# A message-passing graph layer: node features in three DMAs a chunk, loaded three chunks ahead of the stores of h, and the first edge scalars behind the last store

## The chip, the cores and the metric

The kernel runs on one core of one Trainium2 chip. The metric is device time in microseconds (us), from the first to the last instruction with the launch's own share around it; the median of three runs is given with the lowest and the highest. The engines are named as in the profile: PE multiplies matrices, DVE and ACT do elementwise work, POOL here issues gathers, and SP only issues DMAs. SP, ACT and POOL each have a queue of DMAs, and these run on 16 DMA engines.

## The reference

One equivariant graph layer with 12500 nodes and 400000 edges, a residual, and a layer norm over each node's 160 features:

```python
s = node_features[:, :64]; v = node_features[:, 64:].reshape(n, 32, 3); a = node_attr
sc_s = s @ sc_ws * a * _inv(64)
sc_v = jnp.einsum('nci,cd->ndi', v, sc_wv) * a[:, :, None] * _inv(32)
h_s = s @ lin1_ws * a * _inv(64)
h_v = jnp.einsum('nci,cd->ndi', v, lin1_wv) * a[:, :, None] * _inv(32)
hid = jax.nn.silu(edge_scalars @ fc_w1 * _inv(64))
w = hid @ fc_w2 * _inv(64)
w1, w2, w3, w4, w5 = jnp.split(w, [64, 128, 160, 192], axis=-1)
es, ev = h_s[edge_src], h_v[edge_src]            # gathers by edge
e0, e1 = edge_attr[:, :1], edge_attr[:, 1:4]
mid_s = [w1 * es * e0,  w4 * (ev . e1) * _inv(3)]
mid_v = [(w2 * es) e1,  w3 ev e0,  w5 cross(ev, e1) * _inv(2)]
agg = segment_sum(mid, edge_dst) / sqrt(16)
o = agg through lin2_ws, lin2_wv, times a
scalars, gates = silu(pre_s[:, :64]), sigmoid(pre_s[:, 64:96])    # pre = sc + o
x = _layernorm(x + concat([scalars, gates * pre_v]))
```

The edges come sorted by destination. All arithmetic is in float32.

## The kernel before, in words

Constants, then a **node stage**, then an **edge stage** of 782 steps of four tiles (a tile is 128 edges), with the finishing of nodes threaded into it.

The node stage (L252 to L342) computes h, 160 values for each node, and stores it to the table `h_tab` in device memory, from which the edge stage gathers. It goes in chunks of 2048 nodes (`CH`): six whole ones and one of 212. The features come transposed: `xs_t` has 64 rows of scalars, `xv_t` 96 rows of vector components. The tile `xa` holds 64 rows of scalars and the first 64 of the vectors (128 partitions by 2048 nodes); `xz` holds the last 32 rows, with the chunk's four quarters one under another (128 partitions by 512). A chunk loads in eight DMAs on SP's queue: `xa` in two halves of the nodes, each as 64 partitions from `xs_t` (L268) and 64 from `xv_t` (L269), 256 KB each, and `xz` in four of 32 partitions, 64 KB each (L273). All chunks have tiles of their own, so no load waits for a tile. PE multiplies by `l1` and `l1z` (L310, L325), DVE multiplies the products by the nodes' attribute into `ht` (L313, L328; three buffers), and ACT's queue stores `ht` to `h_tab` (L339, and L342 for the last 84 nodes). Ahead of chunk 3, `bases` (L286) turns the first destination of each block of three tiles (`rows`, L247, two DMAs at the front of SP's queue) into window starts `lo`.

The written order on SP is: `rows`; all loads of all chunks; the first source indices and edge attributes (L183, L184); the first chunk of edge scalars `es` (L222, two DMAs of 384 KB); the maps `w1` (L280) and `w2` in five pieces, both twice (L283); then `scs`, `scv` and 19 pieces of `l2` (L351, L118, L372). On ACT: the attribute `at`, `l1`, `l1z` and their scaling (L98 to L125), the stores of h, then all destinations `dt` (L345, 1.6 MB). On DVE, behind the node stage: the scaling of `w2` (L348), `rel` from `dt` and `lo` (L379, L384), and the scalings of `l2`, `scv` and `scs` (L110). In the built program the DMAs of SP and ACT share eight semaphores in turn, so each waits for the landing of the one eight places before it in the scheduled order of both queues.

The edge stage: a step gathers h for four tiles on POOL (L419, an indirect DMA for each tile, into one of four buffers `hg`), makes weights on PE from the edge scalars (L410, L412, L431), multiplies weights and gathered rows on DVE into `pr` (L441, L449), builds the selection from `rel` (L487, L490) and sums by destination on PE (L497). Products of a step need its gather, `hid` and, in DVE's order, `rel` before them.

`manual_schedule` keeps the written order on an engine; DMAs and DVE's scalings of the constants can still be placed among the edge stage's first steps.

Of the kernel before, what the change touches and what calls it, by code (L numbers as in the profile page):

```python
# [10 lines left out]
F32 = mybir.dt.float32  # L11
# [9 lines left out]
P = 128  # L21
S = 64
V = 32
# [5 lines left out]
BT = 3  # L29
# [10 lines left out]
NWT = 224  # L40
# [12 lines left out]
def gnn_kernel(  # L53
# [21 lines left out]
    nc = tc.nc  # L75
    N = x.shape[0]
    NT = attr.shape[1]
# [4 lines left out]
    NB = -(-TT // BT)  # L82
# [11 lines left out]
    in_order = ctx.enter_context(ExitStack())  # L94
    in_order.enter_context(tc.manual_schedule(
        engines={ENG.PE, ENG.DVE, ENG.Activation, ENG.Pool, ENG.SP}))
    at = consts.tile([P, NT], F32, name="at")
    nc.scalar.dma_start(at, attr)  # L98

    l1 = consts.tile([P, P], F32, name="l1")  # L100
    nc.vector.memset(l1, 0.0)
    nc.scalar.dma_start(l1[:S, :S], lin1_ws)
    for i in range(2):
        r = slice(S + i * V, S + (i + 1) * V)
        nc.scalar.dma_start(l1[r, r], lin1_wv)
    scales = [(l1[:S], 1.0 / math.sqrt(S)), (l1[S:], 1.0 / math.sqrt(V))]

    def scale():
        for m, by in scales:
            nc.vector.tensor_scalar_mul(m, m, by)  # L110
        scales.clear()

    def block_diagonal(name, w, n, scale, queue=nc.scalar):
        k = w.shape[0]
        m = consts.tile([n * k, n * k], F32, name=name)
        nc.vector.memset(m, 0.0)
        for i in range(n):
            queue.dma_start(m[i * k:(i + 1) * k, i * k:(i + 1) * k], w)  # L118
        if scale != 1.0:
            scales.append((m, scale))  # L120
        return m

    l1z = block_diagonal("l1z", lin1_wv, 4, 1.0 / math.sqrt(V))
    for m, by in scales:
        nc.scalar.mul(m, m, by)  # L125
    scales.clear()


    rel = consts.tile([P, TT], I16, name="rel")
    rows = consts.tile([1, NB], I32, name="rows")  # L130
    early = consts.tile([1, 1], F32, name="early")
# [58 lines left out]
    def index(t):  # L190
        a0, idx, _ = ahead(t)
        return idx[:, t - a0:t - a0 + 1]
# [13 lines left out]

    ess = {}

    def load_chunk(c):
        if c in ess:  # L210
            return
        t0, halves = chunks[c]
        es = ess[c] = loads.tile([2 * S, SIDE * P], F32, name="es")
        for half, n in enumerate(halves):
            to = es[half * S:(half + 1) * S]
            e0 = (t0 + half * BT) * P
            if n < BT:
                nc.sync.dma_start(to[:, :n * P], es_t[:, e0:e0 + n * P])
                continue
            k = n // BT  # L220
            full = es_t[:, e0:e0 + EB]
            nc.sync.dma_start(  # L222
                to[:, :n * P].rearrange("c (q e) -> c q e", e=EB),
                bass.AP(tensor=full.tensor, offset=full.offset,
                        ap=[full.ap[0], [2 * EB, k], [1, EB]]))
# [16 lines left out]
    nc.gpsimd.iota(share, pattern=[[RATE, NB]], base=0, channel_multiplier=0)  # L242

    even = NB // 16 * 16
    with nc.allow_non_contiguous_dma(reason="the first destination of each block"):
        for b0, b1, outer in ((0, even, 16), (even, NB, 1)):
            nc.sync.dma_start(  # L247
                rows[:, b0:b1].rearrange("o (a b) -> o a b", a=outer),
                dst[0:1, b0 * BT:(b1 - 1) * BT + 1:BT].rearrange("o (a b) -> o a b", a=outer))


    U = 4  # L252
# [2 lines left out]
    CH = 4 * U * P  # L255
    starts = list(range(0, N, CH))
    with tc.tile_pool(name="nodes", bufs=len(starts)) as nodes, tc.tile_pool(
        name="nodes_ps", bufs=6, space=PSUM
    ) as nps, tc.tile_pool(name="z_ps", bufs=2, space=PSUM) as zps:
        loaded = []  # L260
        for c0 in starts:
            cn = min(CH, N - c0)
            quarters = 4 if cn == CH else 1
            assert quarters == 4 or cn <= U * P
            xa = nodes.tile([P, CH], F32, name="xa")
            for b0 in range(0, cn, CH // 2):
                b1 = min(b0 + CH // 2, cn)
                nc.sync.dma_start(xa[:S, b0:b1], xs_t[:, c0 + b0:c0 + b1])  # L268
                nc.sync.dma_start(xa[S:, b0:b1], xv_t[:2 * V, c0 + b0:c0 + b1])  # L269
            xz = nodes.tile([P, U * P], F32, name="xz")  # L270
            cq = cn // quarters
            for q in range(quarters):
                nc.sync.dma_start(xz[q * V:(q + 1) * V, :cq],  # L273
                                  xv_t[2 * V:, c0 + q * cq:c0 + (q + 1) * cq])
            loaded.append((c0, cn, quarters, cq, xa, xz))
        index(0)
        load_chunk(0)
        for half in range(2):
            r = slice(half * S, (half + 1) * S)
            nc.sync.dma_start(w1[r, r], fc_w1)  # L280
            at_c = 0
            for a, b in ((64, 128), (0, 64), (192, 224), (160, 192), (128, 160)):
                nc.sync.dma_start(w2[r, at_c:at_c + b - a], fc_w2[:, a:b])  # L283
                at_c += b - a

        def bases():  # L286

            base_f = ends_pool.tile([1, NB], F32, name="base_f")
            nc.vector.tensor_copy(base_f, rows)
            for b0 in range(0, NB, U * P):  # L290
                b1 = min(NB, b0 + U * P)
                ps = nps.tile([P, U, P], F32, name="hp").rearrange("p u c -> p (u c)")
                nc.tensor.matmul(ps[:, :b1 - b0], ones, base_f[:, b0:b1], start=True, stop=True)
                nc.scalar.copy(lo[:, b0:b1], ps[:, :b1 - b0])
            nc.vector.tensor_sub(share, rows, share)
            nc.vector.tensor_reduce(early, share, AX.X, OP.min)
            nc.vector.tensor_scalar(early, early, -float(MARGIN), None, op0=OP.is_lt)

        for c0, cn, quarters, cq, xa, xz in loaded:
            if c0 == 3 * CH:  # L300
                bases()
            ht = nodes.tile([P, 4 * U, D], F32, name="ht", bufs=3)
            nt = -(-cn // P)
            first = c0 // P
            full = cn // P
            for t0 in range(0, nt, U):
                ps = nps.tile([P, U, P], F32, name="hp")
                for t in range(t0, min(t0 + U, nt)):
                    n = min(P, cn - t * P)
                    nc.tensor.matmul(ps[:n, t - t0], xa[:, t * P:t * P + n], l1,  # L310
                                     start=True, stop=True)
                k = min(U, full - t0)
                nc.vector.tensor_mul(  # L313
                    ht[:, t0:t0 + k, :P], ps[:, :k],
                    at[:, first + t0:first + t0 + k, None].to_broadcast([P, k, P]))
                if t0 + k < nt <= t0 + U:
                    n = cn - full * P
                    nc.vector.tensor_scalar(ht[:n, full, :P], ps[:n, full - t0],
                                            at[:n, first + full:first + full + 1], None, op0=OP.mult)

            pz = zps.tile([P, U, 4, V], F32, name="pz")
            k = quarters * V
            for u in range(-(-cq // P)):
                n = min(P, cq - u * P)
                nc.tensor.matmul(pz[:n, u, :quarters].rearrange("p q c -> p (q c)"),  # L325
                                 xz[:k, u * P:u * P + n], l1z[:k, :k], start=True, stop=True)
            if quarters == 4:
                nc.vector.tensor_mul(  # L328
                    ht[:, :, P:].rearrange("p (q u) c -> p u q c", q=4), pz,
                    at[:, first:first + 4 * U].rearrange("p (q u) -> p u q", q=4)[:, :, :, None]  # L330
                    .to_broadcast([P, U, 4, V]))
            else:
                nc.vector.tensor_mul(ht[:, :full, P:], pz[:, :full, 0],
                                     at[:, first:first + full, None].to_broadcast([P, full, V]))
            if cn > full * P:
                n = cn - full * P
                nc.vector.tensor_scalar(ht[:n, full, P:], pz[:n, full, 0],
                                        at[:n, first + full:first + full + 1], None, op0=OP.mult)
            nc.scalar.dma_start(  # L339
                h_tab[c0:c0 + full * P, :].rearrange("(q p) d -> p q d", p=P), ht[:, :full])  # L340
            if cn > full * P:
                nc.scalar.dma_start(h_tab[c0 + full * P:c0 + cn, :], ht[:n, full])  # L342


    nc.scalar.dma_start(dt, dst)  # L345
    iota = consts.tile([P, W], F32, name="iota")
    nc.vector.tensor_copy(iota, iota_i)
    nc.vector.tensor_scalar_mul(w2, w2, 1.0 / math.sqrt(64))  # L348

    scs = consts.tile([S, V3], F32, name="scs")  # L350
    nc.sync.dma_start(scs, sc_ws)  # L351
# [593 lines left out]
```

## Time and profile before

| | us |
|---|---|
| median of 3 runs | 4070.39 |
| lowest, highest | 4069.28, 4070.66 |
| the profiled execution | 4073.52 |
| its span, first to last instruction | 4071.7 |
| PE busy | 3355.0 (82%) |
| POOL busy | 3011.1 (74%), 3125 gathers in it |
| DVE busy | 2431.4 (60%) |
| ACT busy | 957.8 (24%) |
| DVE's last product of the node stage ends | 71.3 |
| first gather begins | 79.10 |
| first product of the edge stage (L441) begins | 93.93 |

The page gives the busy time of each engine, and for each group of instructions what its engine's idle time before it waited for. A timeline's line is: start, duration, engine, line, operation, tiles, count, and in brackets the idle time before it and what ended that. "SPq" and "ACTq" are the issuing of DMAs on these queues. A DMA's bytes move later than its issue.

### The profile page before, as it was taken

The page shows a single profiled execution, that of the slowest core. Times are in us where ns is not written, and L with a number is a line of the kernel's source. Part 1 is how long each engine was busy: PE and PEld are TensorE (multiplying, and loading weights), DVE is VectorE, ACT ScalarE, POOL GpSimd, SP SyncE. Part 2 cuts the span into 40 slices and gives each one's busy share as a digit, 9 for nine tenths or more (in the row PEclk, how much of TensorE's full clock was granted, in tenths as well). Part 3 has the DMA queues.
Part 4 walks back from the last instruction along what each step waited for, and adds up shares of the span by engine and source line. Part 5 has one row for each costly group of instructions (what it writes and reads, how often), then busy time and mean ns, then how long its engine had stood idle before and what let it go on. Part 6 is the DMA issues. An engine that isn't in the chain of part 4 may idle for free. (4 is left out here: it accounts for less than half of the span.)

```text
span 4071.7 us, 54463 instructions
## 1 busy us (share of the span) xinstructions
PE 3355.0 (82%) x17415; PEld 1636.2 (40%) x17415; DVE 2431.4 (60%) x6367; ACT 957.8 (24%) x3033; POOL 3011.1 (74%) x3133
## 2 busy tenths in 40 slices
PE   5888888887888888888888888888888888888887
PEld 4343443443443433434344343344343343444443
DVE  4655665665655656656656566566565665655655
ACT  0312222221222222222222122122222221221222
POOL 1777777777777777777777777777777777777775
PEclk7989889999998998998999899999899998998988
DMA  8434444444434434434444344344444444444442
GB/s 206 113 90 101 101 97 98 105 93 101 106 91 109 100 91 109 100 90 109 96 94 109 93 100 107 93 101 102 96 101 97 100 101 99 100 100 100 98 97 58
DMA packets 293165, 412.20 MB, mean 101 GB/s; under 512 B 75694, under 2 KB 240442, under 8 KB 292746
## 3 DMA queue, kind: packets, MB, share of 16 engines
q0 software_dynamic: 150000, 256.20, 26.2%
q1 hardware_dynamic: 129592, 142.75, 15.9%
q10 hardware_dynamic: 13282, 9.69, 0.8%
q8 instruction: 143, 2.34, 0.2%
q14 instruction: 148, 1.21, 0.1%
HBM read 392.40 MB, written 16.00 MB: 100 GB/s over the span
## 5 line engine op out<-in xcount | busy, mean ns | idle before, releaser
L419 POOL DMA_INDIRECT hg<-h_tab,idx x3125 | 3009.4, 963 | 1028.5 <-issue 852.5
L441 DVE TENSOR_TENSOR pr<-pw,hg 128x512 f32<-128x512 f32 x782 | 539.3, 690 | 1497.5 <-DMA hg<-h_tab,idx 1191.6
L497 PE MATMUL pa<-pr,sel 128*64 128x416 f32 x6250 | 1407.0, 575 | 2.3 <-DVE sel L490 2.3
L431 PE MATMUL pw<-w,hid 64*128 64x224 f32 x6250 | 873.9, 395 | 481.9 <-DVE oh L487 449.3
L449 DVE TENSOR_TENSOR pr<-pw,hg 128x384 f32<-128x384 f32 x2346 | 1152.7, 546 | 0.1
L431 PEld LDWEIGHTS pw<-w,hid 64*128 64x128 f32 x6250 | 583.3, 197 | 789.5 <-issue 657.9
L497 PEld LDWEIGHTS pa<-pr,sel 128*64 128x64 f32 x6250 | 408.5, 146 | 599.5 <-issue 551.1
L690 ACT COPY sa<-pa 128x416 f32<-128x416 f32 x521 | 263.2, 505 | 1320.9 <-PE pa L497 1315.8
L410 PE MATMUL ph<-es,w 128*128 128x512 f32 (+1 forms) x784 | 466.4, 678 | 28.5 <-DMA w<-in_fc_w_dram 12.9
L412 ACT ACTIVATE hid<-ph 128x512 f32<-128x512 f32 x392 | 233.6, 596 | 765.6 <-PE ph L410 765.0
L490 DVE TENSOR_TENSOR sel<-oh,eas 128x256 f32<-128x256 f32 x782 | 337.9, 432 | 38.1 <-DVE oh L487 0.9
L506 PEld LDWEIGHTS pt<-ident,sa 128*128 128x128 f32 (+1 forms) x2084 | 222.2, 133 | 341.6 <-issue 255.2
L506 PE MATMUL pt<-ident,sa 128*128 128x128 f32 (+1 forms) x2084 | 336.1, 285 | 9.2 <-DVE acc L671 7.0
L522 PE MATMUL po<-tt,l 128*96 128x256 f32 (+3 forms) x1360 | 312.4, 377 | 12.8 <-DVE z L557 11.4
L510 ACT COPY tt<-pt 128x192 f32<-128x192 f32 x521 | 164.6, 316 | 525.3 <-PE pt L506 524.4
L522 PEld LDWEIGHTS po<-tt,l 128*96 128x96 f32 x1360 | 212.1, 164 | 129.5 <-issue 47.7
L410 PEld LDWEIGHTS ph<-es,w 128*128 128x128 f32 x784 | 126.2, 203 | 326.5 <-issue 249.1
L530 DVE TENSOR_TENSOR acc<-acc,os 96x32 f32 x1042 | 193.1, 185 | 24.7 <-ACT os L525 5.4
L487 DVE TENSOR_TENSOR oh<-rel,iota 128x64 f32<-128x64 int16 x782 | 168.7, 216 | 0.0
L556 PE MATMUL pp<-ident,acc 96*128 96x96 f32 x196 | 40.3, 294 | 127.7 <-DVE acc L530 127.0
L525 ACT COPY os<-po 96x512 f32<-96x512 f32 (+2 forms) x68 | 38.3, 564 | 311.9 <-PE po L522 298.7
L512 ACT COPY tt<-pt 128x32 f32<-128x32 f32 x521 | 102.5, 197 | 0.0
(78 smaller groups left out, 781.3 us busy)
## 6 DMA issues: line engine op xcount, KB each, us to landing
es<-in_es_t_dram SPq DMA_DIRECT2D x260, 384.0 KB
hg<-h_tab,idx POOLq DMA_INDIRECT x3125
h_tab<-ht ACTq DMA_DIRECT2D x6, 1280.0 KB
xt<-in_x_dram SPq DMA_DIRECT2D x23, 320.0 KB
out_dram<-y SPq DMA_DIRECT2D x23, 320.0 KB
xv<-in_xv_t_dram SPq DMA_DIRECT2D x25, 187.5 KB
eat<-in_ea_dram SPq DMA_DIRECT2D x30, 120.0 KB
xs<-in_xs_t_dram SPq DMA_DIRECT2D x25, 125.0 KB
```

The lines of the kernel that those rows point to most:

```text
L410: nc.tensor.matmul(ph[:k, c], w1[:k, :k], es[:k, t0 * P + c0 * P:t0 * P + c1 * P], start=True, stop=True)
L412: nc.scalar.activation(hid[:k, c], ph[:k, c], AF.Silu, scale=1.0 / math.sqrt(64))
L419: nc.gpsimd.indirect_dma_start(out=hg[:, t, :], out_offset=None, in_=h_tab, in_offset=bass.IndirectOffsetOnAxis(ap=i, axis=0))
L431: nc.tensor.matmul(pw[:, t, :NWT], hid[r, c * P:(c + 1) * P], w2[r], start=True, stop=True)
L441: nc.vector.tensor_mul(two, pw[:, :n, :2 * S].rearrange("p t (k c) -> p t k c", k=2), hg[:, :n, None, :S].to_broadcast([P, n, 2, S]))
L449: nc.vector.tensor_mul(pr[:, :n, first:first + V3].rearrange("p t (i c) -> p t i c", i=3), pw[:, :n, None, 2 * S + k * V:2 * S + (k + 1) * ...
L490: nc.vector.tensor_mul(sel[:, :n], oh[:, :, None, :].to_broadcast([P, n, 4, W]), by_slot(tiles[0][0])[:, u:u + n, :, None].to_broadcast([P ...
L497: nc.tensor.matmul(pa[half * ROWS:(half + 1) * ROWS, :NPR], sel[:, t].rearrange("p k w -> p (k w)"), pr, start=start, stop=stop)
L506: nc.tensor.transpose(pt[:c, four * P:four * P + k], sa[:k, four * P:four * P + c], ident[:k, :k])
L522: nc.tensor.matmul(po[:, k, :nb], l2[:b, terms[to, part, four]], a[:, :nb], start=(n == 0), stop=(n == len(of) - 1))
L530: nc.vector.tensor_add(window, window, os[:, :, b])
L690: nc.scalar.copy(sa, pas.pop(j)[:, :NPR])
```

## The change

The node stage's loads become a function, `load(c0)`, with three DMAs for each chunk: 64 partitions by 2048 from `xs_t`, 64 by 2048 from `xv_t` (512 KB each), and one of 128 partitions by 512 for `xz` (256 KB), whose side in device memory is an access pattern of 4 quarters by 32 rows by 512 values. Chunk 0 is loaded first of all, ahead of `at`, `l1` and `l1z`; then chunks 1 and 2, then `rows`; in the loop, chunk k + 3 is loaded ahead of the work and the store of chunk k. The first indices and attributes follow the last chunk's loads. `load_maps` loads `fc_w2` whole and twice into a tile `raw`, and DVE scales its five pieces into `w2`. The maps are loaded behind the node stage in the written order, and the first edge scalars go on ACT's queue, behind the last store of h and ahead of `dt`.

```diff
-    at = consts.tile([P, NT], F32, name="at")
-    nc.scalar.dma_start(at, attr)
...
-    l1z = block_diagonal("l1z", lin1_wv, 4, 1.0 / math.sqrt(V))
...
-    def load_chunk(c):
+    def load_chunk(c, queue=nc.sync):
...
-            nc.sync.dma_start(
+            queue.dma_start(
                 to[:, :n * P].rearrange("c (q e) -> c q e", e=EB),
...
-        for c0 in starts:
+
+        def load(c0):
+
             cn = min(CH, N - c0)
             quarters = 4 if cn == CH else 1
             assert quarters == 4 or cn <= U * P
             xa = nodes.tile([P, CH], F32, name="xa")
-            for b0 in range(0, cn, CH // 2):
-                b1 = min(b0 + CH // 2, cn)
-                nc.sync.dma_start(xa[:S, b0:b1], xs_t[:, c0 + b0:c0 + b1])
-                nc.sync.dma_start(xa[S:, b0:b1], xv_t[:2 * V, c0 + b0:c0 + b1])
+            nc.sync.dma_start(xa[:S, :cn], xs_t[:, c0:c0 + cn])
+            nc.sync.dma_start(xa[S:, :cn], xv_t[:2 * V, c0:c0 + cn])
             xz = nodes.tile([P, U * P], F32, name="xz")
             cq = cn // quarters
-            for q in range(quarters):
-                nc.sync.dma_start(xz[q * V:(q + 1) * V, :cq],
-                                  xv_t[2 * V:, c0 + q * cq:c0 + (q + 1) * cq])
+            z = xv_t[2 * V:, c0:c0 + cq]
+            nc.sync.dma_start(xz[:quarters * V, :cq],
+                              bass.AP(tensor=z.tensor, offset=z.offset,
+                                      ap=[[cq, quarters], [z.ap[0][0], V], [1, cq]]))
             loaded.append((c0, cn, quarters, cq, xa, xz))
-        index(0)
-        load_chunk(0)
-        for half in range(2):
-            r = slice(half * S, (half + 1) * S)
-            nc.sync.dma_start(w1[r, r], fc_w1)
-            at_c = 0
-            for a, b in ((64, 128), (0, 64), (192, 224), (160, 192), (128, 160)):
-                nc.sync.dma_start(w2[r, at_c:at_c + b - a], fc_w2[:, a:b])
-                at_c += b - a
+
+        def load_maps():
+
+            raw = ends_pool.tile([2 * S, NWT], F32, name="raw")
+            for half in range(2):
+                r = slice(half * S, (half + 1) * S)
+                nc.sync.dma_start(w1[r, r], fc_w1)
+                nc.sync.dma_start(raw[r], fc_w2)
+            return raw
...
-        for c0, cn, quarters, cq, xa, xz in loaded:
+        load(starts[0])
+        at = consts.tile([P, NT], F32, name="at")
+        nc.scalar.dma_start(at, attr)
...
+        for c0 in starts[1:3]:
+            load(c0)
+        load_bases()
+        for k, c0 in enumerate(starts):
+            if k + 3 < len(starts):
+                load(starts[k + 3])
+            elif k + 3 == len(starts):
+                index(0)
+            _, cn, quarters, cq, xa, xz = loaded[k]
             if c0 == 3 * CH:
                 bases()
...
+    raw = load_maps()
+    load_chunk(0, nc.scalar)
     nc.scalar.dma_start(dt, dst)
     iota = consts.tile([P, W], F32, name="iota")
     nc.vector.tensor_copy(iota, iota_i)
-    nc.vector.tensor_scalar_mul(w2, w2, 1.0 / math.sqrt(64))
+    at_c = 0
+    for a, b in ((64, 128), (0, 64), (192, 224), (160, 192), (128, 160)):
+        nc.vector.tensor_scalar_mul(w2[:, at_c:at_c + b - a], raw[:, a:b], 1.0 / math.sqrt(64))
+        at_c += b - a
```

In the built program of the changed kernel, SP's order behind the last chunk's loads is: indices, attributes, `w1` and `raw` twice, `scs`, the second indices and attributes, the first self-connection loads (`xs2`, `xv2`), `scv`, `l2`, the second chunk of edge scalars. On DVE all scalings of `scv`, `l2` and `scs` stand between `rel` and the first product, where before they were mixed into the products of the first steps. PE's and POOL's orders are unchanged.

More of the change, by code (lines that the diff above doesn't have):

```diff
@@ L96, in gnn_kernel @@
         engines={ENG.PE, ENG.DVE, ENG.Activation, ENG.Pool, ENG.SP}))
-    at = consts.tile([P, NT], F32, name="at")
-    nc.scalar.dma_start(at, attr)
[L100 to L121, printed above, removed]
-    l1z = block_diagonal("l1z", lin1_wv, 4, 1.0 / math.sqrt(V))
-    for m, by in scales:
-        nc.scalar.mul(m, m, by)
-    scales.clear()
     rel = consts.tile([P, TT], I16, name="rel")
@@ L217, in load_chunk @@
             if n < BT:
-                nc.sync.dma_start(to[:, :n * P], es_t[:, e0:e0 + n * P])
+                queue.dma_start(to[:, :n * P], es_t[:, e0:e0 + n * P])
                 continue
@@ L244, in gnn_kernel, with load_bases @@
     even = NB // 16 * 16
[L245 to L249, printed above, removed]
+    def load_bases():
+        with nc.allow_non_contiguous_dma(reason="the first destination of each block"):
+            for b0, b1, outer in ((0, even, 16), (even, NB, 1)):
+                nc.sync.dma_start(
+                    rows[:, b0:b1].rearrange("o (a b) -> o a b", a=outer),
+                    dst[0:1, b0 * BT:(b1 - 1) * BT + 1:BT].rearrange("o (a b) -> o a b", a=outer))
     U = 4
@@ L297, in bases, with scale, block_diagonal @@
             nc.vector.tensor_scalar(early, early, -float(MARGIN), None, op0=OP.is_lt)
-        for c0, cn, quarters, cq, xa, xz in loaded:
+        load(starts[0])
+        at = consts.tile([P, NT], F32, name="at")
+        nc.scalar.dma_start(at, attr)
+        l1 = consts.tile([P, P], F32, name="l1")
+        nc.vector.memset(l1, 0.0)
+        nc.scalar.dma_start(l1[:S, :S], lin1_ws)
+        for i in range(2):
+            r = slice(S + i * V, S + (i + 1) * V)
+            nc.scalar.dma_start(l1[r, r], lin1_wv)
+        scales = [(l1[:S], 1.0 / math.sqrt(S)), (l1[S:], 1.0 / math.sqrt(V))]
+        def scale():
+            for m, by in scales:
+                nc.vector.tensor_scalar_mul(m, m, by)
+            scales.clear()
+        def block_diagonal(name, w, n, scale, queue=nc.scalar):
+            k = w.shape[0]
+            m = consts.tile([n * k, n * k], F32, name=name)
+            nc.vector.memset(m, 0.0)
+            for i in range(n):
+                queue.dma_start(m[i * k:(i + 1) * k, i * k:(i + 1) * k], w)
+            if scale != 1.0:
+                scales.append((m, scale))
+            return m
+        l1z = block_diagonal("l1z", lin1_wv, 4, 1.0 / math.sqrt(V))
+        for m, by in scales:
+            nc.scalar.mul(m, m, by)
+        scales.clear()
+        for c0 in starts[1:3]:
[7 more added lines that the diff above has]
+            _, cn, quarters, cq, xa, xz = loaded[k]
             if c0 == 3 * CH:
```

## The prediction

> **What bounds the kernel now.** I read the page's groups first, then the waits of POOL over the whole span, then its timeline at both ends.
>
> ```profile
> L419 POOL DMA_INDIRECT hg<-h_tab,idx x3125 | 3009.4, 963 | 1028.5 <-issue 852.5
> ...
> POOL hg L419 <- issue: 852.5, 2798, 0.3
> POOL hg L419 <- DMA h_tab<-ht: 76.8, 1, 76.8
> POOL hg L419 <- DMA hg<-h_tab,idx: 34.4, 113, 0.3
> ...
> 79.10 1.10 POOL L419 DMA_INDIRECT hg<-h_tab,idx  x1 [76.75 <-DMA h_tab<-ht]
> 80.50 0.95 POOL L419 DMA_INDIRECT hg<-h_tab,idx  x1 [0.30 <-issue]
> ...
> 4039.35 0.94 POOL L419 DMA_INDIRECT hg<-h_tab,idx  x1 [0.30 <-DVE pr L449]
> ```
>
> PE is the busiest engine by share (82%), yet POOL sets the end: 3125 gathers follow each other with 0.3 us between them, and the longest wait of any kind behind the first is those 0.3 us. The one long wait is the first, 76.8 us for the stores of h. From the first gather (79.10) to the end of the last (4040.3) nothing holds POOL, and 31.4 us of tail follow. So whatever moves the first gather moves the end by as much, and nothing else in the first 80 us counts, unless it later makes POOL wait.
>
> What sets 79.10 is the DMA traffic of the node stage, which I read by windows (time, then engines' busy time, granted clock, DMA share, GB/s) and in the waits of SP's queue up to 110 us.
>
> ```profile
> 2.50:7.00 4.50, 0.00 (x0) 0.00 (x0) 0.04 (x1) 0.00 (x0) 0.00 (x0) 1.00 0.92 37
> 12.00:20.00 8.00, 7.54 (x45) 7.57 (x46) 3.11 (x5) 0.00 (x0) 0.00 (x0) 1.00 1.05 234
> 46.00:49.00 3.00, 3.00 (x19) 3.00 (x18) 1.25 (x2) 0.00 (x0) 0.00 (x0) 0.61 0.12 22
> 53.00:62.00 9.00, 5.26 (x36) 4.80 (x34) 3.46 (x5) 0.00 (x0) 0.00 (x0) 0.81 1.11 334
> 65.00:71.00 6.00, 5.51 (x32) 5.27 (x32) 2.45 (x6) 0.00 (x0) 0.00 (x0) 0.68 0.73 168
> ...
> SPq L268 <- DMA h_tab<-ht: 23.9, 3, 8.9
> SPq L283 <- DMA h_tab<-ht: 8.2, 1, 8.2
> SPq L269 <- DMA l<-in_lin_wv_dram: 5.8, 1, 5.8
> ```
>
> Loads run at 234 GB/s, a stretch of mostly stores at 334. The features are 12500 x 160 x 4 bytes = 8.0 MB in and h is 8.0 MB out: 34.2 + 24.0 us. The first edge scalars (2 x 0.39 MB, L222) take 3.4 us, indices and attributes (0.15 MB) 0.6. That is 62.2 us of full work. The other 16.9 us before the first gather are idle DMA: 8.3 in the first 10 us (0.40 MB moved, worth 1.7 us), 2.8 in 46 to 49 (3 us at 22 GB/s in place of 334), 1.7 in 65 to 71 (6 us at 168 in place of 234), some 2 from the last byte to the gather, 2.1 scattered. SP causes the holes: a load waits for the DMA eight places before it in the built order, and with eight loads a chunk that place is often a store.
>
> **The change, part by part, on the first gather's start.**
>
> *First edge scalars behind the last store.* They leave the path: -3.4 us. They now compete with the first gathers, which move 82 KB each 1.25 us (66 GB/s). Below it is asked whether they are late.
>
> *Destinations of blocks, and the start.* The two DMAs of L247 (1.41 us of SP) no longer stand ahead of the first features, and SP no longer waits 5.8 us at L269: the first chunk's two halves need no earlier DMA in the new order. The first row to bound it is 8.3 us lost; I take -4.5, ends 0 and -6.4 (2.21 to 8.58, from the first load's issue to the second's). Against it, L101's clearing of l1 stands behind the 0.94 us of L240, so PE's first product, at 12.46 waiting for xa, could then wait for l1: the 0 end holds that. Destinations are wanted at 39.41 (L289), 20 us behind their new place.
>
> *Three loads a chunk, three chunks ahead.* Eight DMAs in flight now span two chunks with their stores, and chunk 4 is the first load that must await a store (chunk 1's). The holes at 46 and 65 should close: -4.5, ends 0 and -6.6 (with the scattered 2.1). Joining halves (256 KB to 512 KB) changes no bytes: nothing, hidden in the queue.
>
> *Pulled ahead.* In the built order the second indices and attributes and the first self-connection loads (0.46 MB) now stand ahead of the last two stores, and chunk 6's stores wait for them by semaphore: 0.46 MB at 234 GB/s, +2.0; ends 0 and +4 (a further landing, 2 us).
>
> *The joined z load.* Four loads of 32 partitions become one, whose chip side counts 128 rows and whose memory side counts 4 quarters x 32 rows. On how many engines does it run? The page's row of ACT's queue (packets, MB, share) bears on it, and the DMA view of 40 to 50 us, in quarters of a us:
>
> ```profile
> q10 hardware_dynamic: 13282, 9.69, 0.8%
> ...
> GB/s 229 230 197 246 226 171 191 279 343 353 335 333 333 330 338 340 380 307 312 310 320 251 92 26 23 20 20 18 0 0 0 0 0 0 0 180 164 164 410 295
> ```
>
> ACT's 17 DMAs have 13012 pieces (at 128, l1 and l1z 256, stores 12288 + 128 + 84, destinations 128). 270 remain, which is 16 x 16 + 14 if each engine used posts one more: the 84-row store ran on 14 engines, the largest divisor of its rows up to 16. So row counts decide, and this load has two: by 128 it uses 16 engines, by 4 it uses 4. With four, these engines carry 64 KB of z a chunk in place of 16. In 45.75 to 47 a trickle of some 20 GB/s, a sixteenth of 334, is one straggling engine by itself: 48 KB more is 2.4 us a chunk, 14.4 for six. Against it, the four then lag, and their part of xa (64 KB at 234/16 = 14.6 GB/s, 4.4 us) runs beside idle neighbours at up to 20 GB/s, 3.2 us: -7.2. Net +7; ends 0 (16 engines) and +19.7 (48 KB at 14.6, no relief).
>
> The Trainium skill speaks against the change here: "DMA: Bandwidth & Descriptors", in the section on why a DMA increments its semaphore by 16, says that the number of engines is the largest up to 16 that divides the slowest dimension of both sides. The 14 above agrees, though there both sides had 84 rows. By that rule this load gets 4 engines and the sum is the forecast's; by the row alone 16 is as good a reading, and the sum is the first rival's.
>
> *Maps.* Ten loads of w2 become two of raw, and one product (L348, 0.28 us) five of at most that: DVE +1.1, while it waits for the destinations anyway. Without that cover, 1.1 at the first product.
>
> *What comes late behind the stores.* ACT now issues two edge-scalar loads and then dt, and by its semaphore dt also waits for one of the l2 loads that waits for the last full store: some 2.4 us (two issues, one landing) behind the last store, where before it was issued at 75.61, before the landing. Behind it stand all of DVE's work: rel, then all 20 scalings, now ahead of the first product where before they were mixed into it.
>
> ```profile
> 75.61 0.36 ACTq L345 DMA_DIRECT2D dt<-in_dst_dram  x1
> 86.40 0.28 DVE L348 TENSOR_SCALAR w<-w 128x224 f32<-128x224 f32 x1 [14.99 <-DMA w<-in_fc_w_dram]
> 86.70 7.05 DVE L379 TENSOR_TENSOR rel<-dt,lo 128x520 int16<-128x520 int32 x6
> 93.93 0.67 DVE L441 TENSOR_TENSOR pr<-pw,hg 128x512 f32<-128x512 f32 x1
> 102.29 0.94 POOL L419 DMA_INDIRECT hg<-h_tab,idx  x1 [0.31 <-DVE l L110]
> ```
>
> POOL has four gather buffers: the 17th gather needs the first product done. It is due 23.2 us behind the first gather (102.29 - 79.10), three gathers slowed beside rel included. The new chain, from the landing (1.4 us before the first gather, by POOL's first semaphore event at 77.7): 2.4, then 7 (1.6 MB at the 313 GB/s of 77 to 82, plus 2 for start and landing) to 11.1 (75.61 to 86.70), rel 7.5, scalings 4.6, product 2.4: 22.5 to 26.6 behind the first gather. A wait of 0 to 3.4 us, once. I take 0, as dt's bytes decide and L348 held rel before.
>
> **Sum.** 79.1 - 3.4 - 4.5 - 4.5 + 2.0 + 7.0 = 75.7: the first gather 3.4 us earlier. The profiled execution took 4073.5 (span 4071.7) and would take 4070.1; the median of the runs is 3.1 below it, so 4070.4 - 3.4 = 4067.0 us.
>
> **Rivals.** *The z load spreads over 16 engines.* First gather at 68.7 (the sum without the 7.0), 4060.0 us; with the far ends of start and holes and none of the 2.0 pulled ahead, 62.7 and 4054. For it: the 128 rows it writes, and that 270 shows a count of rows, not which side's. Against it: the 4.
>
> *The four z engines become the stage's bound.* Every chunk waits for the slowest engine, so the holes stay: 79.1 - 3.4 - 4.5 + 2.0 + 19.7 = 92.9, 4084.2 us, slower. It decides from the point where the four engines cost over 5.9 us while the holes stay (1.0 a chunk), or 10.4 where they close (1.7 a chunk); at 20 GB/s without relief they cost 2.4 a chunk. For it: loads at 14.6 GB/s an engine when all run. Against it: that rate belongs to 16 engines writing 64 partitions, not to four.
>
> *Late destinations give the gain back.* POOL waits 3.4 us before its 17th gather: 4070.4, no change. It decides where the first product ends over 23.2 us behind the first gather.
>
> **How the numbers follow.** Forecast 0.40, 16 engines 0.36, four engines as the bound 0.18, late destinations 0.06. What a measurement of this kernel tells from no change is about 0.2%, 8.1 us. Faster by more: 0.29 of the 16-engine case, and 0.13 of the forecast's, where the relief or the closed holes bring more: 0.42. Slower by more: 0.13 of the bound, 0.02 of the forecast's, 0.01 of late destinations: 0.16. The rest is 0.42. Range 4055 to 4078: the bottom is nearly the 16-engine case's best, the top holds half of the way into the four-engine bound. The forecast's own range is 4058 to 4074.
>
> **What would show it.** The first gather's start is the measure: 76 forecast, 63 to 69 with 16 engines, over 79 with the bound. The waits of SP for h_tab should shrink from 32 us, the window 2.5 to 7 fill up, and 46 to 49 hold no hole. Four engines show as a DMA rate near 80 GB/s (4 x 20) in stretches of the loads with the share far under 1. POOL should have no second wait over 0.3 us; one near the 17th gather is the destinations. It would all be wrong if POOL's step of 1.25 us changed.

## The result, and the profile after

The changed kernel takes 4083.88 us (median of 7 runs, 4081.34 to 4086.76) beside 4070.39 (4068.63 to 4075.97) for the kernel before in the same session: ratio 1.0033, 95% interval 1.0023 to 1.0043. It is slower by 13.5 us; 4067.0 was forecast, with 4078 as the top of the range. The profiled execution took 4083.88, its span is 4082.0 (before: 4071.7).

First the waits of POOL over the whole span: engine, tile, line, what it waited for, total us, times, longest.

```profile
POOL hg L434 <- issue: 857.8, 2816, 0.3
POOL hg L434 <- DMA h_tab<-ht: 86.0, 1, 86.0
POOL hg L434 <- DMA hg<-h_tab,idx: 33.2, 109, 0.3
POOL hg L434 <- DVE oh L502: 20.6, 53, 4.8
```

The first wait grew from 76.8 to 86.0 us, and there is a second one that is not 0.3 but 4.8. POOL's timeline places both:

```profile
88.38 1.10 POOL L434 DMA_INDIRECT hg<-h_tab,idx  x1 [86.03 <-DMA h_tab<-ht]
...
114.89 0.94 POOL L434 DMA_INDIRECT hg<-h_tab,idx  x1 [4.76 <-DVE oh L502]
...
4048.97 1.04 POOL L434 DMA_INDIRECT hg<-h_tab,idx  x1 [0.30 <-DVE oh L502]
```

The first gather starts at 88.38 in place of 79.10 (+9.3), and the 17th waits 4.76 us for the first products (the name in the bracket is the last of DVE's instructions by then). The last gather starts 9.6 us later than before. 13.7 us were lost and 4.1 came back on the way, mostly as shorter gathers: the busy time of the group L434 is 3005.6 us, that of L419 before was 3009.4. The step of 1.25 us is the same.

The windows of the node stage (time, busy time of PE, its weight loads, DVE, ACT and POOL, clock, DMA share, GB/s) show where the 9.3 us lie:

```profile
2.50:7.00 4.50, 0.00 (x0) 0.00 (x0) 0.06 (x1) 0.00 (x0) 0.00 (x0) 1.00 0.89 207
25.50:28.00 2.50, 2.50 (x25) 2.50 (x24) 1.53 (x3) 0.00 (x0) 0.00 (x0) 0.99 0.48 80
31.00:34.00 3.00, 1.15 (x5) 1.18 (x6) 0.00 (x0) 0.00 (x0) 0.00 (x0) 0.73 0.25 80
```

The start did fill: 207 GB/s from 2.5 to 7 us, where there were 37. But at 31 to 34 the DMA engines are busy a quarter of the time and move 80 GB/s: four of sixteen, 20 GB/s each, the sign that the forecast named. (25.5 to 28 is on the way there.) The waits of SP's queue up to 110 us, and ACT's queue:

```profile
SPq L238 <- DMA h_tab<-ht: 14.5, 1, 14.5
SPq L243 <- DMA h_tab<-ht: 13.5, 1, 13.5
SPq L243 <- DMA l<-in_lin_ws_dram: 6.5, 1, 6.5
```

```profile
19.64 24.60 ACTq L349 DMA_DIRECT2D h_tab<-ht  x3
44.29 1.15 ACT L265 COPY lo<-hp 128x512 f32<-128x512 f32 x3 [34.35 <-DMA h_tab<-ht]
```

Store 0 is issued at 19.64, and store 2 waits for its landing: the group of three stores ends at 44.2. A store of 1.3 MB thus needed some 24 us. The reading, which e1, e3 and e4 test: a quarter of its data goes through the four engines that also carry z, and it lands when those are done. The semaphore events of the trace, sixteen for each store, agree. Twelve of store 0's come at 27.2 to 28.7 us, the last four at 42.3 to 43.3, and store 2 is issued at 43.39. Store 1's come at 42.8 to 44.5 and 48.1 to 49.3, and chunk 4's loads, which waited 14.5 us for it, go at 49.34; store 3's come at 65.1 to 66.4 and 71.6 to 72.6, and chunk 6's z load, after 13.5 us, goes at 72.58.

The length of these waits is not the four engines' alone. In e1 below, with z on 16 engines, all sixteen events of store 0 come at 34.3 to 36.5, the last 19.8 us behind its issue, and SP's two long waits are 14.7 and 11.1 us; in the kernel before, store 0 landed 6.6 us behind its issue. So the stores are slower in the new order too, where more loads are queued ahead of them; no run parts this from the row load that now stands beside store 0.

The end of the stage, from the timelines of ACT and DVE (two views):

```profile
85.69 0.60 ACTq L352 DMA_DIRECT2D h_tab<-ht  x1
86.33 1.80 ACTq L190 DMA_DIRECT2D es<-in_es_t_dram  x2
93.20 0.36 ACTq L357 DMA_DIRECT2D dt<-in_dst_dram  x1
```

```profile
77.89 0.24 DVE L347 TENSOR_SCALAR ht<-pz,at 84x32 f32<-84x32 f32 x1
...
101.00 7.14 DVE L394 TENSOR_TENSOR rel<-dt,lo 128x520 int16<-128x520 int32 x6 [17.45 <-DMA dt<-in_dst_dram]
...
108.44 3.97 DVE L284 TENSOR_SCALAR l<-l 32x96 f32<-32x96 f32 x20
112.43 0.20 DVE L284 TENSOR_SCALAR scs<-scs 64x96 f32<-64x96 f32 x1
112.55 0.68 DVE L456 TENSOR_TENSOR pr<-pw,hg 128x512 f32<-128x512 f32 x1
```

DVE finishes h at 78.1, the last store is issued at 85.7, dt at 93.2 (75.61 before). rel starts at 101.0, the scalings follow, and the first products end at 114.6, 26.2 us behind the first gather, where the prediction allowed 23.2.

### The profile page after: what moved, and what is told of

Read it like the earlier page. It is cut to its first block, busy times and chain, and to the rows that moved or that the text cites. A ratio compares the mean times of both kernels' runs of the same rounds, so it can differ in the third digit from the quotient of the medians.

```text
span 4082.0 us, 54404 instructions
## 1 busy us (share of the span) xinstructions
PE 3348.4 (82%) x17415; PEld 1632.8 (40%) x17415; DVE 2432.9 (60%) x6371; ACT 957.2 (23%) x3033; POOL 3007.3 (74%) x3133
## 3 DMA queue, kind: packets, MB, share of 16 engines
q0 software_dynamic: 150000, 256.20, 26.2%
## 5 line engine op out<-in xcount | busy, mean ns | idle before, releaser
L434 POOL DMA_INDIRECT hg<-h_tab,idx x3125 | 3005.6, 962 | 1042.1 <-issue 857.8
```

Of the source, the lines that this page charges most:

```text
L434: nc.gpsimd.indirect_dma_start(out=hg[:, t, :], out_offset=None, in_=h_tab, in_offset=bass.IndirectOffsetOnAxis(ap=i, axis=0))
```

## The experiments

Theory 1: the joined z load runs on four engines. Theory 2: the new order makes stores and loads wait for each other, whatever z runs on. Theory 3: dt comes late. Theory 4 came later: the load of `rows`, and not an idle queue, costs most of the first 7 us. Sessions ran on several chips, so a time is read only against the kernel before on the same chip.

**e1, the changed kernel with z on 16 engines.** The memory side of the z load counts rows first and quarters second, and `l1z` is laid out to match:

```diff
-    ap=[[cq, quarters], [z.ap[0][0], V], [1, cq]]
+    ap=[[z.ap[0][0], V], [cq, quarters], [1, cq]]
...
-                queue.dma_start(m[i * k:(i + 1) * k, i * k:(i + 1) * k], w)
+                rows_of = slice(i, n * k, n) if name == "l1z" else slice(i * k, (i + 1) * k)
+                queue.dma_start(m[rows_of, i * k:(i + 1) * k], w)
```

> The changed kernel with one difference: the joined z load of a chunk lays its rows out as (row, quarter), so that its memory side counts 32 rows x 4 quarters x 512 and the chip side 128 rows; number of DMAs, bytes, queues and order are those of the changed kernel. Theory 1 (the joined z load ran on four engines, and these delayed the stores): the stretches with a DMA share near 0.25 at 80 to 105 GB/s vanish, the first gather starts at 64 to 74 us in place of 88.4, and the median falls by 10 to 20 us against the changed kernel's 4083.9, to 4062 to 4074; the 4.8 us wait before the 17th gather may stay. Theory 2 (the new order of loads, whose semaphores wait for stores, delays the stores whatever the z load runs on): first gather 84 to 90, median 4079 to 4085. Theory 3 (the late destinations alone are the loss): first gather unchanged at 88, wait before the 17th gather unchanged, median unchanged.

First gather 76.71, 11.7 us earlier than in the changed kernel; the wait of 4.76 stays. Time 4070.23 against 4069.28 for the kernel before (1.0001, 0.9992 to 1.0010). The same windows as above, in this kernel:

```profile
25.50:28.00 2.50, 2.50 (x25) 2.50 (x24) 1.38 (x2) 0.00 (x0) 0.00 (x0) 1.00 1.10 161
31.00:34.00 3.00, 2.14 (x6) 1.09 (x6) 2.74 (x4) 0.00 (x0) 0.00 (x0) 0.88 1.01 303
```

Neither stretch falls to a quarter here. Theory 1 holds for most of the loss; but 76.71 lies above its 64 to 74, so something else is missing.

**e2, the changed kernel with four z loads a chunk again.**

```diff
+    for q in range(quarters):
+        nc.sync.dma_start(xz[q * V:(q + 1) * V, :cq], xv_t[2 * V:, c0 + q * cq:c0 + (q + 1) * cq])
```

> The changed kernel with the z load of a chunk as four loads of 32 partitions again, as before the change; everything else of the change stays. This also moves every later DMA to another semaphore (six DMAs a chunk in place of three). Theory 1 (four engines): first gather 66 to 78 us, median 4064 to 4076. Theory 2 (order and semaphores): first gather 80 to 90, since the stores and loads still wait for one another, median 4076 to 4085.

First gather 81.04 and a wait of 3.3 us before the 17th; 4073.66 (1.0008, 0.9999 to 1.0017). The time is as theory 1 has it, the gather as theory 2: with six DMAs a chunk SP waits 30.2 us for stores at the z loads. The run does not separate the theories.

**e3 and e4, the join alone in the kernel before**, with its memory side as in the change (e3) and rows first (e4).

> The kernel before, with one part of the change alone: the z load of a chunk joined into one as in the change (memory side 4 quarters x 32 rows). Theory 1 (four engines): the profile gets stretches near 80 to 105 GB/s with a DMA share near 0.25, the first gather moves from 79.1 to between 84 and 95, and the kernel is 5 to 16 us slower than the kernel before. Theory 2 (order, not engines): first gather 78 to 81, time within 3 us of the kernel before.

> The kernel before, with the z load of a chunk joined into one whose memory side counts 32 rows x 4 quarters, as in the first of these runs. Against the run before it, only the order of the rows of the z load differs. Theory 1 (four engines): no stretch at 80 to 105 GB/s with a low share, first gather 74 to 80, time 0 to 5 us under the kernel before, and 5 us or more under the run with 4 quarters x 32 rows. Theory 2: as that run, within 2 us.

| | first gather | time | before | ratio, 95% interval |
|---|---|---|---|---|
| e3, 4 quarters x 32 rows | 89.11 | 4079.05 | 4069.28 | 1.0020 (1.0011 to 1.0029) |
| e4, 32 rows x 4 quarters | 74.30 | 4063.46 | 4069.28 | 0.9987 (0.9978 to 0.9996) |

The order of two counts in the z load's access pattern differs, and with it only the layout of `l1z` and the place of the last chunk's z rows. 20 to 30 us, e3 and then e4:

```profile
20.00:30.00 10.00, 7.49 (x48) 7.14 (x48) 3.85 (x7) 0.00 (x0) 0.00 (x0) 0.83 0.87 228
```

```profile
20.00:30.00 10.00, 8.45 (x72) 8.06 (x72) 7.73 (x12) 0.00 (x0) 0.00 (x0) 1.00 1.08 293
```

From 31 to 33 us e3 moves 93 GB/s at a share of 0.27, e4 333 at 1.14. 14.8 us of first gather and 15.6 us of time hang on it: theory 1 is shown, without anything else of the change. Joining the z loads is a gain where all engines take part: 5.8 us of time, more than the 0 to 5 expected. The Trainium skill's "DMA: Bandwidth & Descriptors", in the section on why a DMA increments its semaphore by 16, takes the largest divisor up to 16 of both sides' slowest dimensions. By that rule e3 has 4 engines and e4 16, and both runs agree (shares of 0.27 and 1.14).

**e5 and e10, e1's kernel with dt ahead of the first edge scalars on ACT's queue.** e5's chip granted PE a clock of 0.83 and took 5145 us for the kernel before; e10 is the same kernel on another chip.

```diff
-    load_chunk(0, nc.scalar)
     nc.scalar.dma_start(dt, dst)
+    load_chunk(0, nc.scalar)
```

> The changed kernel with the 32 rows x 4 quarters z load (as e1_after_z16: first gather 76.71, wait of 4.76 us before the 17th gather, median 4070.2) and one more difference: the destinations dt are issued on ACT's queue ahead of the first edge scalars, directly behind the last store of h. Theory 3 (what comes late behind the stores holds POOL at its 17th gather: dt was issued at 81.38, 7.5 us behind the tail store): dt is issued at about 75, rel starts some 5 to 6 us earlier, the wait of 4.76 falls to 0.3 to 1, and the median falls by 3 to 5 us, to 4065 to 4067.5. Rival (rel is held by the bytes of dt and the 20 scalings, not by the issue; or the edge scalars, now behind dt, hold PE's first products in its place): wait of 3 to 5 us stays, median 4068 to 4072. First gather 76 to 77.5 by both.

> The kernel of e5_z16_dt_first once more (the changed kernel with the 32 rows x 4 quarters z load, dt issued ahead of the first edge scalars), on another chip. Theory 3 (the wait before the 17th gather is the late issue of dt): wait of 0.3 to 1.5 us in place of e1_after_z16's 4.76, first gather 75 to 77.5, median 2 to 5 us under the kernel before. Rival (the late edge scalars hold PE and so the first product): wait 3 to 5 us, median within 2 us of the kernel before.

e5: first gather 75.58, no wait before the 17th gather (1.1 us before the 21st), ratio 0.9989 (0.9970 to 1.0007), too wide to tell. e10: 4084.12 against 4087.53 (0.9992, 0.9983 to 1.0001). Its first and 17th gathers:

```profile
75.39 1.10 POOL L438 DMA_INDIRECT hg<-h_tab,idx  x1 [73.05 <-DMA l<-in_lin_wv_dram]
...
96.74 1.07 POOL L438 DMA_INDIRECT hg<-h_tab,idx  x1 [0.30 <-DVE oh L506]
```

dt is issued at 73.56 in place of e1's 81.38, and the wait is gone. Theory 3 holds for the wait. Against the kernel before, e1 lost 1.0 us and e10 gained 3.4, about the wait's 4.5; but the two intervals overlap, so the times alone don't show that it reaches the end.

**e6 to e9, single parts of the change in e4's kernel:** the edge scalars behind the last store and ahead of dt (e6), `xa` in two loads (e7), the loads of `rows` behind those of chunk 2 (e8, and e9 on another chip).

> The kernel before with the z load joined over 32 rows x 4 quarters (as e4_before_z16: first gather 74.30, median 4063.5) and one part of the change: the first edge scalars go on ACT's queue behind the last store of h and ahead of dt. The prediction's term for this part: first gather -3.4 us (to 71), 0 us from late destinations. Theory of a gain given back: first gather 70 to 73, but dt is issued 3 to 7 us later than the 69.07 of that run, so a wait of 1 to 5 us comes before the 17th gather: median 4060 to 4064. If the waits of the last stores set the first gather, not the bytes: first gather 73 to 75 and the median 4063 to 4068.

> The kernel before with the z load joined over 32 rows x 4 quarters (as e4_before_z16: first gather 74.30, median 4063.5) and one part of the change: the two halves of xa joined, so that a chunk loads in three DMAs of 512, 512 and 256 KB. All loads stay ahead of everything in SP's written order. The prediction's term for this part: the holes between loads close, first gather 70 to 73, median 4059 to 4062. Rival (eight DMAs in flight then hold whole chunks, and a load that waits for the eighth before it waits for a store of 1.3 MB: SP waits of 10 us and more for h_tab at chunks 4 and 6, as the 14.7 and 11.1 of e1_after_z16): first gather 75 to 79, median 4064 to 4069.

> The kernel before with the z load joined over 32 rows x 4 quarters (as e4_before_z16: first gather 74.30, median 4063.5) and one part of the change: the two loads of the blocks' first destinations go behind the loads of chunk 2, so that the first loads of features are the first of SP's queue. The prediction's term for this part: -4.5 us (0 to -6.4) on the first gather: 68 to 74, median 4057 to 4063. Rival (a wait for the weights' small loads, some 6 us, stays in SP's queue one DMA further on, and the start's gain is eaten by later waits for stores): first gather 73 to 75.5, median 4062 to 4065.

> The kernel of e8_joined_start once more (the kernel before, with the z load joined over 32 rows x 4 quarters and the blocks' first destinations loaded behind chunk 2), since the chip of that run granted PE a clock of 0.83 and all its kernels took 5134 us and more. Where the granted clock is near 0.92, as in the first four runs: first gather 70 to 72 (70.45 there), no wait over 0.3 us behind it, and a median 7 to 13 us under the kernel before, 2 to 5 us under e4_before_z16's 5.8. Rival (the first gather differs from chip to chip by as much): first gather 73 to 76, median 4 to 7 us under the kernel before.

| | first gather (e4: 74.30) | wait before the 17th | ratio, 95% interval |
|---|---|---|---|
| e6, late edge scalars | 72.36 | 4.95 | 0.9985 (0.9963 to 1.0006) |
| e7, joined xa | 72.81 | none | 0.9991 (0.9973 to 1.0009) |
| e8, rows later | 70.45 | none | 0.9984 (0.9964 to 1.0003) |
| e9, as e8 | 73.03 | none | 0.9978 (0.9969 to 0.9987) |

e6 to e8 ran on the chip of e5, so their ratios decide nothing; the node stage can be compared, with a granted clock like the others' there. e6 moves the first gather up by 1.9 us and brings the whole wait of the changed kernel: the edge scalars ahead of dt are its cause. e7 gives 1.5 where the prediction's term was 4.5. e8 and e9 are one kernel, and their first gathers differ by 2.6 us from chip to chip: 3.9 and 1.3 earlier than e4's. e9's 73.03 lies outside its 70 to 72, and its gain over the kernel before, 8.7 us, inside its 7 to 13; that is 2.9 above e4's, on different chips. Single parts gain a little each in e4's kernel, yet e1, which has them all, has its first gather 2.4 us behind e4's 74.30. What e1 adds, loads three chunks ahead among the stores and small loads ahead of the last ones, was not tried singly.

**e11, one queue.** e1's kernel with loads, stores, dt and edge scalars all on SP's queue in written order, the maps ahead of the store of chunk 4, dt directly behind the last store, `l1z` loaded on SP behind chunk 0:

```diff
-            nc.scalar.dma_start(
+            nc.sync.dma_start(
                 h_tab[c0:c0 + full * P, :].rearrange("(q p) d -> p q d", p=P), ht[:, :full])
...
-    raw = load_maps()
-    load_chunk(0, nc.scalar)
-    nc.scalar.dma_start(dt, dst)
+    nc.sync.dma_start(dt, dst)
+    load_chunk(0)
```

> The changed kernel with the 32 rows x 4 quarters z load and with every DMA up to the edge stage on SP's queue, in the written order: loads of chunk k + 3, store of chunk k; the first indices and the maps ahead of the store of chunk 4; behind the last store dt, then the first edge scalars, then the rest; the loads of l1z on SP behind those of chunk 0. So no store waits for a load that was issued behind a wait for an earlier store, and each waits for the one eight places before it in its own queue. Theory 2 (the last stores were held by the small loads that the two-queue order puts between them, 66.05 to 73.91 in e1_after_z16): the last store is issued within 2 us of DVE's last product, first gather 62 to 70, a wait of 0 to 4 us before the 17th gather, median 9 to 17 us under the kernel before. Rival (the bytes set the time, and the waits only hid it): first gather 71 to 76, median 0 to 7 us under.

First gather 73.23, no second wait; 4082.37 against 4087.53 (0.9984, 0.9975 to 0.9993). The forecast of 62 to 70 failed. Its window of 20 to 30 us says why, and the DMA view of the same stretch (packets, bytes, rate, and packets by size):

```profile
20.00:30.00 10.00, 6.96 (x58) 6.42 (x57) 5.90 (x10) 0.00 (x0) 0.00 (x0) 1.00 1.05 132
```

```profile
DMA packets 1364, 1.32 MB, mean 132 GB/s; under 512 B 1108, under 2 KB 1108, under 8 KB 1236
```

The engines are full (share 1.05) and move 132 GB/s, with 1108 packets under 512 B, most of them the 1042 single values of `rows`. The kernel before has them in its first 7 us, in the window that the prediction showed (share 0.92, 37 GB/s). Its DMA view from 2.5 to 7 us, and SP's queue in it split at 3.2 us (2.2 to 3.2, then 3.2 to 7):

```profile
DMA packets 872, 0.17 MB, mean 37 GB/s; under 512 B 837, under 2 KB 837, under 8 KB 872
...
q1 hardware_dynamic: 744, 0.15, 89.8%
```

```profile
q1 hardware_dynamic: 1053, 0.00, 55.9%
```

```profile
q1 hardware_dynamic: 35, 0.14, 96.2%
```

SP's queue alone fills 89.8% of 16 engines with 744 packets. To divide that time evenly among them (87 ns each, as e12's expectation does) misreads it: from 2.2 to 3.2 us the 1053 packets, nearly all of the row, take 0.559 x 16 x 1 us / 1053 = 8.5 ns each, and then 35 packets of 4 KB of the first features take 0.962 x 16 x 3.8 us / 35 = 1.7 us each. In e12, below, where the row is whole, 198 packets from 3.2 to 7 us at 74.5% take 0.23 us each. So the features behind the row are held up, for some 4 us; by what in the engines is not shown. That the row's load costs this time is theory 4.

**e12 to e14, the row whole:** one contiguous DMA of 12.5 KB, and one DVE copy that picks every third value; in the kernel before (e12), in e9's (e13) and in e11's (e14).

```diff
+    nc.sync.dma_start(firsts.rearrange("o (a b) -> o a b", a=4),
+                      dst[0:1, :NFD].rearrange("o (a b) -> o a b", a=4))
...
+            nc.vector.tensor_copy(rows, firsts[:, ::BT])
```

> The kernel before with one difference: the first destinations of the blocks, 1042 values of 4 bytes with a stride of 12 in device memory, come as one contiguous row of 12.5 KB (one DMA of 3124 values), and DVE picks every third value into rows in one copy of 1 x 1042. Theory 4 (the prediction took the first 10 us of the kernel before for idle DMA, 8.3 us lost to SP's waits; but 744 of the row's packets of 4 bytes filled 89.8% of all 16 engines from 2.5 to 7 us, some 87 ns of one engine each, so some 5 us of that time is the row load itself and moves with it): the window 2.5 to 7 fills with features, the first gather comes 3 to 6 us earlier, at 73 to 76, and the median is 3 to 6 us under the kernel before. Rival (the time was SP's wait for the weights' landing, 5.8 us, and stays): first gather 78 to 80, median within 2 us of the kernel before.

> The kernel of e9_joined_start_again (the kernel before with the z load joined over 32 rows x 4 quarters and the first destinations behind chunk 2; first gather 73.03, 8.7 us under the kernel before) with the first destinations as one contiguous row of 12.5 KB, every third value picked by DVE. Theory 4: the stretch of 4-byte packets at 30 to 40 us (166 GB/s in that run) goes, first gather 67 to 70, median 11 to 15 us under the kernel before. Rival (other transfers or waits hide the row there): first gather 72 to 74, median 7 to 10 us under.

> The kernel of e11_one_queue (all DMAs of the node stage on SP's queue; first gather 73.23, 5.2 us under the kernel before) with the first destinations as one contiguous row of 12.5 KB, every third value picked by DVE. Theory 4: the stretch at 20 to 30 us with a DMA share of 1.05 at 132 GB/s goes to 230 and more, first gather 66 to 70, a wait of 0 to 2 us before the 17th gather, median 8 to 13 us under the kernel before. Rival (the bytes or the landing of the last stores set the end): first gather 71 to 74, median 4 to 7 us under.

| | first gather | time | before | ratio, 95% interval |
|---|---|---|---|---|
| e12, before | 72.85 | 4085.82 | 4091.52 | 0.9988 (0.9979 to 0.9997) |
| e13, e9's | 67.70 (e9: 73.03) | 4077.16 | 4091.52 | 0.9966 (0.9952 to 0.9979) |
| e14, e11's | 67.12 (e11: 73.23) | 4077.18 | 4091.52 | 0.9966 (0.9954 to 0.9978) |

In e12 the row's single values are gone from 2.5 to 7 us (SP's queue, first line); e14 moves 253 GB/s at 20 to 30 us, where e11 had 132:

```profile
q1 hardware_dynamic: 199, 0.68, 62.9%
```

```profile
20.00:30.00 10.00, 6.95 (x58) 6.38 (x57) 7.61 (x11) 0.00 (x0) 0.00 (x0) 1.00 1.02 253
...
60.00:67.00 7.00, 0.00 (x0) 0.00 (x0) 0.00 (x0) 0.59 (x1) 0.00 (x0) 0.50 1.13 326
```

5.3 to 6.3 us of first gather in three kernels, each against a run on another chip, wherever the load stood: theory 4 holds. In e12 SP's second load is issued at 3.48 in place of 8.58, so e12 alone doesn't part the row from SP's wait at L269; e13 and e14 do, since e9 and e11 issue theirs at 1.40 already. The skill's page named above says in "Rules for kernel authors" that a strided last dimension becomes one descriptor for each element; the 1053 packets above agree. e13 and e14 differ in their queues and end alike. In its last 7 us before the gather e14 moves 326 GB/s, near the 334 of the stores before the change, so its bytes set the end; e13 moves 188 at a share of 0.87, so there that isn't shown. Theory 2 keeps a part: e1's first gather is 3.5 us behind e11's, which differs in queues and order (another chip). Both e13 and e14 beat the two kernels: they are 14 us faster than the kernel before, the changed one 13.5 slower, on their own chips.

## Why the prediction was wrong

The mechanism that bounds the kernel was read rightly: the first gather sets the end, and a new wait of POOL adds to it. The first gather came 12.7 us later than the sum had it (88.38 for 75.7), and the wait before the 17th gather adds 4.5.

Three steps failed: the price of the z load, the gains from the start, the holes and the edge scalars, and the late destinations taken as 0.

*The joined z load.* Four engines were expected; +7.0 was taken for them, as 14.4 us for 48 KB a chunk at 20 GB/s less a relief of 7.2, since the four would read their part of xa faster beside idle neighbours. Measured: 11.7 (the changed kernel against e1) and 14.8 (e3 against e4), near the 14.4, and most of the relief is not seen. Against four separate loads the join cost 10.0 us in the kernel before (e3's 89.11 less 79.10) and 7.3 in the changed one (less e2's 81.04); that 7.0 lies so near is partly luck, since the sum also left out that joining on 16 engines gains 4.8 (e4, on another chip than the 79.10). So the rival "the four z engines become the stage's bound" came true, and SP still waited 30 us for stores, where 32 had been. Its 4084.2 us met the measured 4083.88 by luck: the first gather came 4.5 us before its 92.9, and the wait before the 17th gather gave 4.5 back.

*The start*, -4.5, rested on a wrong reading of a shown line. The window of 2.5 to 7 us was called idle because it moved 37 GB/s; its share stands beside that, 0.92. SP's wait at L269 was real, but most of the time behind it was the row load's: it holds up what follows wherever it stands. Moving it past three chunks, among loads and stores, gained 1.3 (e9) to 3.9 (e8). "1.41 us of SP" was its issue; what it holds up, 5 to 6 us, was never priced.

*Three loads, holes closed*, -4.5: e7 shows 1.5 for joined xa; three chunks ahead was not tried alone. *Edge scalars behind the stores*, -3.4: e6 shows 1.9. Both are differences of single profiles from different chips. Of the 12.7 us, 4.7 are the z load (11.7 less 7.0) and 8.0, the larger part, these three terms and the pulled-ahead loads together (e1's 76.71 for the first rival's 68.7). Against those 8.0 stand 6.1 for the row (e11 less e14) and 3.5 for the two queues' order and the start together (e1 less e11); how the 8.0 divide among the terms stays open.

*Late destinations*, taken as 0 of 0 to 3.4 us: 4.5 beyond the usual 0.3. The chain was to end 22.5 to 26.6 us behind the first gather and ended 26.2 behind it, inside; but the 17th gather was due 22.05 behind (109.18 + 0.95 + 0.30, less 88.38) and not 23.2, as two gathers were slowed in place of three. And one part was mis-sized: the issue of dt, put at 2.4 us behind the last landing (by the prediction 1.4 us before the first gather, 86.98), came 6.2 behind it. dt's issue to rel's start (7.8), rel (7.3), scalings (4.2) and products (2.1) lay at or under their sizes. With 2.4 for the 6.2, the wait would have been under 1 us, by these numbers. Both signs were on the page: the two edge-scalar loads ahead of dt, and its wait for an l2 load that itself waits for the last store. The term's chance as a rival, 0.06, treated it as an alternative; it added to the four engines instead.

*Maps and pulled-ahead loads* weren't tried singly. DVE's five pieces (L362) ended at 83.5, long before dt.

## What to carry to other kernels

Before joining DMAs, read the slowest dimension of both access patterns: where it had 4 entries, 12 engines stood idle, and the stores that shared the four landed 15 us late in part. Read DMA share and GB/s together: a full share at 37 GB/s is no idle time; here moving the row load behind it gained 1.3 to 3.9 us, and loading the row whole 5.3 more (e13). When loads go behind the last store, follow each queue's issue order to the first instruction that needs the last of them.

## What the runs showed of the hardware

- DMAs on four engines moved 20 GB/s for each of them (80 GB/s at a share of 0.25). Of a 1.3 MB store on all engines beside them, twelve engines' parts landed by 28.7 us and the four others' by 43.3; with z on 16 engines (e1) all landed within 2.2 us of each other.
- 1042 single values of 4 bytes cost 5.3 to 6.3 us of the stage (e12 to e14). Their packets take 8.5 ns each; the time stands in the trace as 4 KB packets behind them that take 1.7 us in place of 0.23.
- A 16 KB weight issued at 2.46 us beside two 512 KB loads of chunk 0 (e1) kept SP waiting 6.6 us, until 8.62.
- The kernel before took 4069, 4088, 4092 and 5145 us on four chips. On the last, with a granted clock of 0.83, POOL waited 1088 us for DVE (e8's profile) and no longer sets the pace alone; why was not followed up.
